# Seven products of a layer added up in shared PSUM banks, and relu, bias and residual in one VectorE instruction

## The chip, the cores and the metric

The kernel runs on one core of one Trainium2 chip. The metric is the device time of one execution in microseconds (us). One more execution is recorded by the profiler, and all views come from that one.

## The reference

There are 32 batches of 512 channels by 1024 nodes. Layer 0 is a graph attention, layer 1 a linear map over the channels; each has a residual and a layernorm over the 1024 nodes.

```python
q = einsum('c,bcn->bn', wq, x);  k = einsum('c,bcn->bn', wk, x)
scores = q[:, None, :] + k[:, :, None]
scores = where(scores > 0, scores, 0.01 * scores)
att = softmax(scores, axis=-1)
agg = einsum('bcn,bmn->bcm', x, att)
y = relu(einsum('oc,bcm->bom', adj, agg) + bm[None, :, None])
x = layernorm(x + y, axis=-1)                 # layer 0
W = adj * adj
x = layernorm(x + einsum('bnf,nm->bmf', x, W) + bias, axis=-1)   # layer 1
```

## The kernel before

**Layer 0 without a 1024 x 1024 softmax.** The leaky relu makes a score's exponential one of two products, depending on whether q + k is positive. If the nodes are sorted by q, a node needs one prefix sum and one suffix sum of weighted columns. Per batch the kernel does this:

- `project` multiplies `x` by the weights in eight steps of 128 nodes (matmuls `zp`, L274); ACT copies each result to `zrow` (L262).
- `peak` and `spread` find the largest q (L287, L305) and spread q over all partitions by eight transposes (L298) and one more, `mx` (L302).
- `place` finds each node's rank by comparing with all others (`lt`, L331) and turns ranks to row numbers `ranki` (L336); `send` scatters the rows to a table in DRAM in the order of q (indirect DMA of POOL, L341). `count` finds each node's place for -k on ACT (L356).
- `fetch` reads the sorted rows back to `zs` (DMA, issued by SP, L389). `weigh` builds weights (`w`, L403, and `lq`, L411). `table` forms prefix and suffix sums in nine steps: PE (`tp`, L431), an ACT copy (`ts`, L436), one-row copies of carried sums back to `zs` by POOL (L440) and by ACT (L442), and stores of `ts` to DRAM by SP. A step needs the row that the step before copied.
- `pick` gathers for each node its row of the table (indirect DMA of POOL, L452) to `rows`; `shares` works out its mixing factors (from L471); `scale` (ACT, L498) and `gain` (DVE, L506) mix the three parts.
- `turn` transposes the result on PE (`op`, L544); ACT adds the bias and takes the relu (L548) to `y`; `add` adds the residual `x` on DVE (L553); `stats` (L515), `root` (POOL, L523, L524), `shift` (L530) and `apply` (ACT, L536) are the layernorm.

**Layer 1 by seven products.** W (with the identity for the residual) and Y, the output of layer 0, are cut into 2 x 2 quarters, and seven products of quarters take the place of eight. The sums of weight quarters S1 to S4 are made once. Those of Y are made per batch by `sums` (L589): T1 = Y12 − Y11, T2 = Y22 − T1, T3 = Y22 − Y12, T4 = Y21 − T2. The output's upper rows (tiles 0 and 1) are called `u`, its lower ones `v`, the column halves `lo` and `hi`:

- 11 (`u` lo) = A11·Y11 + A12·Y21
- 12 (`u` hi) = A11·Y11 + S2·T2 + S1·T1 + S4·Y22
- 22 (`v` hi) = A11·Y11 + S2·T2 + S3·T3 + S1·T1
- 21 (`v` lo) = A11·Y11 + S2·T2 + S3·T3 + A22·T4

Each product is two parts `m` of 128 rows, each of two fp32 matmuls over 128 x 512 (L605). It fills two PSUM banks, one tile of the pool `ps_mm` that has three. VectorE (DVE) adds the products up as they come, 128 x 512 at a time (L617), with the bias in the first reads: 18 reads per batch in nine kinds, of which `u4` and `22` read no PSUM. The bias of the right half has that of the left half subtracted, since the left half's sums carry it on.

**The order.** It is written out by hand, every engine runs its instructions in that order, and semaphores join them. A slot `s` works on four batches: `project` for batch s+2, the table for s+1, `turn` and layer 1 for s, the output's layernorm and stores for s−1. After the projection `phase(s)` follows: layer 1 of `s`, with ranks and sends of s+2, the last table step and the gathers of s+1 between its parts. `mul[0]` to `mul[13]` are the fourteen half products on PE in the order A11, S1, S2, S3, A22, S4, A12. POOL's transfers go p0 p1 s0 s1 p2 p3 s2 s3 p4 p5 s4 s5 p6 s6 s7 p7 (p a gather, s a send), then SP issues the fetch. The first and last batches have orders of their own (`begin`, `opening`, `end`). In the last two batches the sums T4 (of 30) and T3, T4 (of 31) and one kind of addition (of 31) run on POOL.

Buffers: `x` has 12 tiles of 128 x 1024, `y` four and `v`, the output before it is stored, four. The tiles of `v` for tiles 2 and 3 of the old batch are normalised and stored at the beginning of `phase`, and are filled again by the batch of that slot. T1 to T4 lie in parts of `rows` that are free at the time.

Of the kernel before, what the change touches and what calls it, by code (L numbers as in the profile page):

```python
# [23 lines left out]
def gat_gcn_resnorm_kernel(  # L24
# [11 lines left out]

# [18 lines left out]
    xpool = ctx.enter_context(tc.tile_pool(name="xpool", bufs=12))  # L89
    tpool = ctx.enter_context(tc.tile_pool(name="tpool", bufs=3))  # L90
    ypool = ctx.enter_context(tc.tile_pool(name="ypool", bufs=4))
    vpool = ctx.enter_context(tc.tile_pool(name="vpool", bufs=4))
# [16 lines left out]
    vec = const.tile([3 * CT, P], F32, name="vec")  # L109
# [4 lines left out]
    bm_sb = const.tile([P, CT], F32, name="bm_sb")  # L114
# [44 lines left out]
    xs = {}  # L159
    kept = {}  # L160

    def load(b, ct):
        xt = xpool.tile([P, N], F32, name=f"x_{b}_{ct}", tag="x")
        nc.sync.dma_start(out=xt, in_=x[b, ct * P : (ct + 1) * P, :])
        xs.setdefault(b, []).append(xt)
# [26 lines left out]
    def turn_weights():  # L192
# [4 lines left out]
        nc.vector.tensor_copy(bm_sb, pt[:, 2 * CT : 3 * CT])  # L197
# [17 lines left out]
    def square_weights():  # L215


        nc.vector.tensor_tensor(w1, adj_sb, adj_sb, ALU.mult)
        for ct in range(CT):
            nc.vector.tensor_tensor(  # L220
                w1[:, ct, ct * P : (ct + 1) * P], w1[:, ct, ct * P : (ct + 1) * P], ident, ALU.add
            )
        nc.vector.tensor_tensor(ws[:, 0], a21, a22, ALU.add)
        nc.vector.tensor_tensor(ws[:, 1], ws[:, 0], a11, ALU.subtract)
        nc.vector.tensor_tensor(ws[:, 2], a12, ws[:, 1], ALU.subtract)
        nc.vector.tensor_tensor(a21, a11, a21, ALU.subtract)
        nc.vector.tensor_tensor(bias_bc[:, hi], bias_bc[:, hi], bias_bc[:, lo], ALU.subtract)
# [11 lines left out]
    room = {  # L239
        ("T1", 0): (5, 2), ("T2", 0): (5, 0), ("T2", 1): (5, 1),  # L240
        ("T1", 1): (6, 0), ("T3", 1): (6, 2), ("T3", 0): (6, 1),
        ("T4", 0): (7, 0), ("T4", 1): (7, 2),
    }

    info = {}
    ys = {}
    vs = {}
# [18 lines left out]
    def project(b, nt, part, kept=True):  # L266
# [5 lines left out]
        for ct in range(part * CT // 2, (part + 1) * CT // 2):  # L272
            for h in range(2):
                nc.tensor.matmul(  # L274
                    zp[:, h, 0:CE],
                    xb[ct][:, nt * P : (nt + 1) * P],
# [16 lines left out]
    def spread(b, to="lq"):  # L293
# [13 lines left out]
        if to == "v":  # L307
            qs = vpool.tile([P, N], F32, name=f"qs_{b}", tag="v")
# [15 lines left out]
    def place(b, *some):  # L324
# [10 lines left out]
        n0, n1 = some[0], some[-1] + 1  # L335
# [164 lines left out]
    def gain(b, some):  # L500

        g, ra = mixes[b]
        for k in some:
            u = g[:, k, 1, 1 : C + 1]
            for i in (2, 0):
# [3 lines left out]
            us.setdefault(b, []).append(u)  # L509
# [30 lines left out]
    def turn(b, ot, pool=ps_mm):  # L540
# [6 lines left out]
        t = ypool.tile([P, N], F32, name=f"y_{b}_{ot}", tag="y")  # L547
        nc.scalar.activation(t, op, AF.Relu, bias=bm_sb[:, ot : ot + 1])  # L548
        ys.setdefault(b, []).append(t)

    def add(b, ot):
        t = ys[b][ot]
        nc.vector.tensor_tensor(t, t, xs[b][ot], ALU.add)  # L553

    def settle(b, ot):
# [3 lines left out]
        stats((0, b, ot), ys[b][ot])  # L559
# [7 lines left out]
    def quarter(b, name, a):  # L567

        if b < B - 2:
            k, u = room[name, a]  # L570
            return rows[:, k, u * ZW : u * ZW + H]
        if (b, name) not in kept:
            kept[b, name] = vpool.tile([P, N], F32, name=f"{name}_{b}", tag="v")
        return kept[b, name][:, a * H : (a + 1) * H]

    def sums(b, *some):

        yt = ys[b]
        for name, a in some:
            t, t1 = quarter(b, name, a), quarter(b, "T1", a)  # L580
            t2 = quarter(b, "T2", a) if name in ("T2", "T4") else None
            y1, y2 = yt[a], yt[CT // 2 + a]
            of, less = {
                "T1": (y1[:, hi], y1[:, lo]), "T2": (y2[:, hi], t1),
                "T3": (y2[:, hi], y1[:, hi]), "T4": (y2[:, lo], t2),
            }[name]
            on_pool = ("T4",) if b == B - 2 else ("T3", "T4") if b == B - 1 else ()
            by = nc.gpsimd if name in on_pool else nc.vector
            by.tensor_tensor(t, of, less, ALU.subtract)  # L589

    def layer1(b):


        yt = ys[b]

        def part(name, a):
            if name[0] == "Y":
                return yt[(CT // 2) * (name[1] == "2") + a][:, lo if name[2] == "1" else hi]
            return quarter(b, name, a)

        def make(w, y, m, some=range(CT // 2)):
            if 0 in some and (m == 0 or b == B - 1 and w in ("S4", "A12")):
                ops[b, w] = ps_mm.tile([P, 2, H], F32, name=f"o{w}_{b}_{m}", tag="mm")
            for a in some:
                nc.tensor.matmul(  # L605
                    ops[b, w][:, m, :], quarters[w][:, a, m * P : (m + 1) * P], part(y, a),
                    start=(a == 0), stop=(a == CT // 2 - 1),
                )

        def read(mt, half, w, m, *of):  # L610
            if (b, mt) not in vs:
                pool, tag = (xpool, "x") if b >= B - 2 else (vpool, "v")
                vs[b, mt] = pool.tile([P, N], F32, name=f"v_{b}_{mt}", tag=tag)
            x0 = ops[b, w][:, m, :] if w else vs[b, mt][:, half]
            x1 = bias_bc[:, half] if not of else vs[b, of[0]][:, of[1]]
            by = nc.gpsimd if b == B - 1 and not w and half is hi and of[1] is lo else nc.vector
            by.tensor_tensor(vs[b, mt][:, half], x0, x1, ALU.add)  # L617

        mul, get = [], {}
        for w, y in (  # L620
            ("A11", "Y11"), ("S1", "T1"), ("S2", "T2"), ("S3", "T3"),
            ("A22", "T4"), ("S4", "Y22"), ("A12", "Y21"),
        ):
            for m in range(2):
                mul.append(lambda *some, w=w, y=y, m=m: make(w, y, m, *some))
        for m in range(2):
            u, v = m, 2 + m
            for name, what in (
                ("c1", (u, lo, "A11", m)),
                ("c5", (v, hi, "S1", m)),  # L630
                ("u2", (u, hi, "S2", m, u, lo)),
                ("u3", (v, lo, "S3", m, u, hi)),
                ("u4", (u, hi, None, m, v, hi)),
                ("22", (v, hi, None, m, v, lo)),
                ("21", (v, lo, "A22", m, v, lo)),
                ("12", (u, hi, "S4", m, u, hi)),
                ("11", (u, lo, "A12", m, u, lo)),
            ):
                get[name, m] = lambda what=what: read(*what)

        def reads(*names):
            for name in names:
                for m in range(2):
                    get[name, m]()

        return mul, get, reads

    def stats1(b, *some):
        for mt in some:
            stats((1, b, mt), vs[b, mt])  # L650
# [13 lines left out]
    def store(b, mt):  # L664
        nc.sync.dma_start(out=out[b, mt * P : (mt + 1) * P, :], in_=vs.pop((b, mt)))

    def rest(b, after):

        mul, get, reads = layer1(b)
        names = (("c1",), ("c5",), ("u2",), ("u3", "u4", "22"), ("21",), ("12",), ("11",))  # L670
        for i in range(len(mul)):
            mul[i]()
            if i == 0:
                shift(0, b, CT - 1)
                apply(0, b, CT - 1)
                sums(b, ("T2", 0), ("T2", 1), ("T3", 0), ("T3", 1), ("T4", 0), ("T4", 1))
            for name in names[i // 2]:
                if b == B - 1 and i > 9:
# [381 lines left out]
```

## Time and profile before

| | |
|---|---|
| device time, three runs | 2321.87, 2324.4, 2327.32 us; median 2324.4 |
| profiled execution: span | 2323.5 us, 30952 instructions |
| PE busy | 2206.9 us, 95% |
| PE weight load busy | 1388.3 us, 60% |
| DVE busy | 2003.3 us, 86% |
| ACT busy | 1403.0 us, 60% |
| POOL busy | 1042.8 us, 45% |
| DMA | 548.68 MB, mean 236 GB/s |
| mean granted PE clock | 0.978 |

The profiled execution's own time is its span, 2323.5 us, from its first to its last instruction. Busy shares are averages over the whole execution, with an opening of some 160 us and an end of about the same length in which engines wait for each other. A group's mean duration counts an instruction from start to end; neighbours on an engine overlap a little, so what an instruction costs its engine is the distance from one start to the next.

### The profile page before, as it was taken

To read this page: it belongs to the slowest core of one execution; us is meant where nothing else is said; L and a number is where in the kernel's file an instruction comes from. 1 tells how busy PE (TensorE), PEld (TensorE's weight loads), DVE (VectorE), ACT (ScalarE), POOL (GpSimd) and SP (SyncE) were. 2 spreads that over 40 slices of the span, in tenths; PEclk is the share of its full clock that TensorE was granted. 3 is DMA by queue.
4 is the path that set the end of the run, shared out by engine and by line. 5 is a ranking of instruction groups with operands and counts; after the bars stand their busy time and mean duration, and the time that the engine had idled before them with its cause. 6 is when DMAs were issued, how large, how long until landed. Compare 5 with 4: busy or idle time off the path is not lost.

```text
span 2323.5 us, 30952 instructions
## 1 busy us (share of the span) xinstructions
PE 2206.9 (95%) x9521; PEld 1388.3 (60%) x9521; DVE 2003.3 (86%) x4153; ACT 1403.0 (60%) x2185; POOL 1042.8 (45%) x1296
## 2 busy tenths in 40 slices
PE   8969999999999999999999999999999999999775
PEld 7636666566665656666656665656666665666332
DVE  4278989888998988899988898998899888889777
ACT  2665566666556667566667556666656666755543
POOL 2424444544444544444453444454444454444433
PEclk9979999999999999999999999999999999999877
DMA  6657878777878777787877787877777877777741
GB/s 250 200 165 238 261 239 280 245 222 235 252 242 265 257 230 231 241 263 248 270 238 220 239 257 240 274 257 224 227 248 253 260 257 231 227 239 248 235 164 73
DMA packets 175421, 548.68 MB, mean 236 GB/s; under 512 B 24748, under 2 KB 24760, under 8 KB 175256
## 3 DMA queue, kind: packets, MB, share of 16 engines
q1 hardware_dynamic: 117888, 277.18, 40.3%
q0 software_dynamic: 57344, 269.52, 33.2%
q8 instruction: 76, 1.25, 0.2%
q14 instruction: 89, 0.73, 0.1%
q10 hardware_dynamic: 24, 0.01, 0.0%
HBM read 338.17 MB, written 208.43 MB: 235 GB/s over the span
## 4 chain that ended last, share of the span: by engine, by line
DVE 42%; DMA 19%; PE 16%; issue 7%; POOL 6%; ACT 6%; SPq 2%; POOLq 0%; DVEq 0%; ACTq 0%
DVE lt L331 12%; DVE v L617 9%; DMA zs<-td 8%; PE zp L274 8%; DVE st L515 6%; PE tp L431 5%; DMA td<-zrow,ranki 5%; DMA rows<-td,idx 4%; DVE rows L589 4%; DVE rows L506 3%; DVE y L553 2%; POOL td L341 2%; PE op L544 2%; DMA td<-ts 2%; SPq L389 2%
## 5 line engine op out<-in xcount | busy, mean ns | idle before, releaser
L274 PE MATMUL zp<-wmT,x 128*128 128x257 f32 x4096 | 947.7, 383 | 1.4 <-ACT zrow L262 1.3
L274 PEld LDWEIGHTS zp<-wmT,x 128*128 128x128 f32 x4096 | 757.5, 190 | 163.4 <-issue 36.8
L440 POOL COPY zs<-ts 1x513 f32<-1x513 f32 x251 | 191.2, 762 | 676.3 <-ACT ts L436 675.3
L431 PE MATMUL tp<-zs,lq 128*64 128x257 f32 x2304 | 333.2, 404 | 63.5 <-DVE lq L411 24.8
L506 DVE SCALAR_TENSOR_TENSOR rows<-rows,ra 128x512 f32<-128x512 f32 x512 | 379.4, 762 | 11.7 <-ACT rows L498 2.5
L452 POOL DMA_INDIRECT rows<-td,idx x256 | 291.9, 1140 | 204.0 <-issue 115.8
L341 POOL DMA_INDIRECT td<-zrow,ranki x256 | 279.0, 1090 | 119.7 <-DVE ranki L336 46.6
L331 DVE SCALAR_TENSOR_TENSOR lt<-qb,zrow,first 128x1024 int8<-128x1024 f32 x240 | 307.1, 1280 | 4.3
L474 ACT ACTIVATE ac<-s 128x4 f32<-128x4 f32 x64 | 13.3, 208 | 486.4 <-DVE s L473 387.9
L431 PEld LDWEIGHTS tp<-zs,lq 128*64 128x64 f32 x2304 | 153.3, 140 | 224.6 <-POOL zs L440 82.5
L356 ACT ACTIVATE sg<-lq,kc 128x1024 int8<-128x1024 f32 x240 | 275.1, 1146 | 6.8
L605 PE MATMUL oA<-y,adj_sb 128*128 128x512 f32 x512 | 243.8, 609 | 11.0 <-ACT y L536 9.9
L436 ACT COPY ts<-tp 128x514 f32<-128x514 f32 x288 | 168.4, 585 | 110.5 <-PE tp L431 85.5
L605 PE MATMUL oS<-rows,ws 128*128 128x512 f32 x480 | 210.9, 591 | 0.0
L498 ACT ACTIVATE rows<-rows,ra 128x512 f32<-128x512 f32 x256 | 166.8, 711 | 55.7 <-DVE ra L485 50.2
L262 ACT COPY zrow<-zp 128x514 f32<-128x514 f32 x256 | 144.8, 577 | 84.1 <-PE zp L274 76.6
L523 POOL TENSOR_SCALAR rs<-mv 128x1 f32<-128x1 f32 x256 | 88.6, 346 | 237.7 <-DVE mv L517 140.6
L553 DVE TENSOR_TENSOR y<-y,x 128x1024 f32<-128x1024 f32 x128 | 156.1, 1219 | 45.1 <-ACT y L548 45.1
L536 ACT ACTIVATE y<-y,nb,rs 128x1024 f32<-128x1024 f32 x128 | 158.5, 1238 | 54.5 <-DVE nb L530 53.2
L524 POOL TENSOR_TENSOR rs<-rs,mhalf 128x1 f32<-128x1 f32 x256 | 180.4, 705 | 21.4
L515 DVE BATCH_NORM_STATS2 st<-y 128x6 f32<-128x512 f32 x256 | 163.8, 681 | 2.7 <-issue 0.2
L605 PEld LDWEIGHTS oA<-y,adj_sb 128*128 128x128 f32 x512 | 94.1, 195 | 120.5 <-issue 98.1
(119 smaller groups left out, 2640.5 us busy)
## 6 DMA issues: line engine op xcount, KB each, us to landing
x<-in_x_dram SPq DMA_DIRECT2D x128, 512.0 KB
out_dram<-v SPq DMA_DIRECT2D x126, 512.0 KB
td<-ts SPq DMA_DIRECT2D x512, 120.5 KB
zs<-td SPq DMA_DIRECT2D x64, 602.3 KB
zs<-td SPq DMA_DIRECT2D x64, 240.9 KB
zs<-td SPq DMA_DIRECT2D x96, 120.5 KB
td<-ts SPq DMA_DIRECT2D x64, 96.4 KB
td<-zs SPq DMA_DIRECT2D x8, 514.0 KB
```

Source lines behind the costliest of these rows:

```text
L274: nc.tensor.matmul(zp[:, h, 0:CE], xb[ct][:, nt * P : (nt + 1) * P], wmT[:, ct, h * CE : (h + 1) * CE], start=(ct == 0), stop=(ct == CT - 1),)
L331: nc.vector.scalar_tensor_tensor(lt, qs, zrow[:, nt, 0:1], first[:, o : o + N], ALU.subtract, ALU.is_lt, accum_out=rank[:, nt : nt + 1],)
L341: sc = nc.gpsimd.indirect_dma_start(out=td[:, :], out_offset=bass.IndirectOffsetOnAxis(ap=ranki[:, nt : nt + 1], axis=0), in_=zrow[:, nt, ...
L356: nc.scalar.activation(sg, qs, AF.Sign, bias=kc[:, nt : nt + 1], accum_out=sgn[:, nt : nt + 1])
L431: nc.tensor.matmul(tp[i * G : (i + 1) * G, h, 0:CE], lw[:, ks[i], :], zs[:, j, h * CE : (h + 1) * CE], start=True, stop=True,)
L440: by.tensor_copy(zs[0:1, to, 1:ZW], ts[0:1, 1:ZW])
L452: nc.gpsimd.indirect_dma_start(out=rows[:, mt, :], out_offset=None, in_=tds[b].rearrange("(s u) c -> s (u c)", u=3), in_offset=bass.Indire ...
L506: nc.vector.scalar_tensor_tensor(u, g[:, k, i, 1 : C + 1], ra[:, k, i : i + 1], u, ALU.mult, ALU.add)
L515: nc.vector.bn_stats(st[:, h, :], t[:, h * H : (h + 1) * H])
L553: nc.vector.tensor_tensor(t, t, xs[b][ot], ALU.add)
L605: nc.tensor.matmul(ops[b, w][:, m, :], quarters[w][:, a, m * P : (m + 1) * P], part(y, a), start=(a == 0), stop=(a == CT // 2 - 1),)
L617: by.tensor_tensor(vs[b, mt][:, half], x0, x1, ALU.add)
```

## The change

Products that are needed together are added in PSUM. Bank pair A takes A11·Y11, then S2·T2, S3·T3 and A22·T4 on top; B takes S1·T1, then S4·Y22; C takes A12·Y21. DVE reads a partial sum between two products, so the next product on the pair waits for that read. Each of the seven reads spans both parts (128 x 2 x 512): `p1` (A), `p5` (B), `u2` (A), `22` (A), `12` (B), `11` (C), `21` (A). The order on PE becomes A11, S1, S2, S4, S3, A12, A22. The sums T1 to T4 are one instruction each over two row tiles (128 x 2 x 512); T3 overwrites Y12 and T4 overwrites Y11. The subtraction of the left half's bias is gone.

ACT's relu (L548) is gone. DVE computes max(op, −bm) + x from PSUM in one instruction; this is relu(op + bm) + x less bm, and bm, one number for a row of 1024 nodes, is taken out by the layernorm's mean.

`gain` does one of its two mixing steps for all tiles and then the other. `x`, `y` and `v` are single tiles of the same size in place of pools. In `phase` the ranks, sums, reads and gathers are put in another order: POOL's transfers now go p0 p1 s0 s1 p2 p3 s2 s3 p4 s4 s5 p5 s6 s7 p6 p7. All of the last batches' sums and additions run on DVE.

```diff
     def gain(b, some):
         g, ra = mixes[b]
-        for k in some:
-            u = g[:, k, 1, 1 : C + 1]
-            for i in (2, 0):
+        for i in (2, 0):
+            for k in some:
+                u = g[:, k, 1, 1 : C + 1]
                 nc.vector.scalar_tensor_tensor(
                     u, g[:, k, i, 1 : C + 1], ra[:, k, i : i + 1], u, ALU.mult, ALU.add
                 )
...
     def turn(b, ot, pool=ps_mm):
...
-        nc.scalar.activation(t, op, AF.Relu, bias=bm_sb[:, ot : ot + 1])
-        ys.setdefault(b, []).append(t)
+        tops[b, ot] = op
     def add(b, ot):
-        t = ys[b][ot]
-        nc.vector.tensor_tensor(t, t, xs[b][ot], ALU.add)
+        nc.vector.scalar_tensor_tensor(
+            yall[:, ot], tops.pop((b, ot)), nbm[:, ot : ot + 1], xs[b][:, ot], ALU.max, ALU.add
+        )
...
     def sums(b, *some):
-        for name, a in some:
...
-            by.tensor_tensor(t, of, less, ALU.subtract)
+        for name in some:
             of, less = {
+                "T1": ("Y12", "Y11"), "T2": ("Y22", "T1"), "T3": ("Y22", "Y12"), "T4": ("Y21", "T2"),
             }[name]
+            nc.vector.tensor_tensor(part(b, name), part(b, of), part(b, less), ALU.subtract)
     def layer1(b):
+        def make(w, y, at, first, m, some=range(CT // 2)):
+            if 0 in some and first and m == 0:
+                ops[b, at] = ps_mm.tile([P, 2, H], F32, name=f"o{at}_{b}", tag="mm")
             for a in some:
                 nc.tensor.matmul(
+                    ops[b, at][:, m, :], quarters[w][:, a, m * P : (m + 1) * P],
+                    part(b, y)[:, a, :], start=first and a == 0, stop=a == CT // 2 - 1,
+                    skip_group_check=not first,
                 )
+        def read(at, of, half, seen, m=None):
+            to, o = v[:, row[of], half], ops[b, at]
+            more = to if seen else bias_bc[:, half].unsqueeze(1).to_broadcast([P, 2, H])
+            if m is not None:
+                to, o, more = to[:, m, :], o[:, m, :], more[:, m, :]
+            nc.vector.tensor_tensor(to, o, more, ALU.add)
+        for of in (
+            ("A11", "Y11", "A", True), ("S1", "T1", "B", True), ("S2", "T2", "A", False),
+            ("S4", "Y22", "B", False), ("S3", "T3", "A", False), ("A12", "Y21", "C", True),
+            ("A22", "T4", "A", False),
+        ):
...
+            "p1": ("A", "u", lo, False), "p5": ("B", "v", hi, False), "u2": ("A", "u", hi, False),
+            "12": ("B", "u", hi, True), "22": ("A", "v", hi, True), "11": ("C", "u", lo, True),
+            "21": ("A", "v", lo, False),
...
     def phase(s, mid, new, old):
...
         mul[1]()
         pick(mid, 0)
         pick(mid, 1)
-        rank(0, 1)
+        rank(0)
+        mul[2]()
+        mul[3]()
+        sums(s, "T2")
+        read("p1")
+        rank(1)
         send(new, 0)
         send(new, 1)
-        sums(s, ("T2", 0), ("T2", 1))
-        mul[2]()
-        mul[3]()
         pick(mid, 2)
         pick(mid, 3)
-        get["c1", 0]()
-        rank(2, 3)
+        mul[4]()
+        mul[5]()
+        rank(2)
+        read("p5")
+        rank(3)
         send(new, 2)
         send(new, 3)
         if new < B - 1:
             pick(mid, 4)
-        sums(s, ("T3", 0), ("T3", 1))
-        get["c1", 1]()
-        mul[4]()
-        mul[5]()
-        sums(s, ("T4", 0), ("T4", 1))
+        mul[6]()
+        mul[7]()
+        sums(s, "T3")
+        rank(4)
+        read("u2")
+        mul[8]()
+        mul[9]()
+        rank(5)
+        send(new, 4)
+        send(new, 5)
         if new < B - 1:
             pick(mid, 5)
-        reads("c5")
-        rank(4, 5)
-        send(new, 4)
-        send(new, 5)
-        mul[6]()
-        mul[7]()
+        rank(6)
+        rank(7)
+        send(new, 6)
+        send(new, 7)
+        sums(s, "T4")
         if new < B - 1:
             pick(mid, 6)
-        reads("u2")
-        rank(6, 7)
-        send(new, 6)
-        send(new, 7)
-        mul[8]()
-        mul[9]()
-        if new < B - 1:
             pick(mid, 7)
         fetch(new)
-        reads("u3", "u4", "22")
         mul[10]()
         mul[11]()
-        reads("21")
+        read("22")
         mul[12]()
         mul[13]()
+        read("12")
+        read("11")
         shares(mid, 0, NT // 2)
         scale(mid, range(NT // 2))
-        reads("12")
+        read("21")
         gain(mid, (0, 1))
-        reads("11")
         gain(mid, (2, 3))
```

## The prediction

> **What bounds the kernel now.** I read the table of stretches first, then the waits, the groups, and last one slot's timeline on TensorE (PE) and VectorE (DVE). Four steady stretches of 72.6 us (core 0; then span, busy us and instructions of PE, PEld, DVE, ACT, POOL; clock, DMA share, GB/s):
>
> ```profile
> 1000.00:1072.60 72.60, 72.29 (x309) 44.80 (x308) 66.71 (x137) 44.21 (x70) 36.00 (x44) 1.00 0.79 252
> 1072.60:1145.20 72.60, 72.50 (x310) 44.90 (x309) 66.36 (x140) 43.63 (x68) 35.64 (x44) 1.00 0.79 259
> 1145.20:1217.80 72.60, 70.17 (x305) 43.85 (x305) 64.05 (x137) 43.60 (x69) 34.00 (x43) 1.00 0.78 245
> ```
>
> PE is busy for 97 to 100% at full clock; DVE, which the change relieves, for about 91%. So a gain in a slot can only come from PE's gaps. I measured those from one slot's `mx` transpose (L302) to the next: 29 slots last 68.93 us in the mean. Adding the shortest time that each group of PE instructions ever took gives 67.57, so 1.36 us per slot is all that can be won, 39 us in the run. The waits (engine, line, releaser; us in total, times, longest) name the gaps:
>
> ```profile
> POOL rows L452 <- DMA td<-ts: 67.0, 16, 4.8
> ...
> DVE y L553 <- ACT y L548: 45.1, 48, 3.8
> ...
> PE tp L431 <- DVE lq L411: 24.8, 24, 8.5
> PE tp L431 <- POOL zs L440: 23.3, 37, 3.0
> ```
>
> Per slot, that is 0.39 us before the table's first step (it needs `lq`), 0.43 at its eighth and 0.14 at its fifth (they need POOL's copy of one row to `zs`), 0.24 in layer 1, and crumbs. The relu wait of 45 us stands on DVE, not on PE: it costs only what it passes on.
>
> **The skill and this trace.** (1) "VectorE: DVE Perf Modes", section on the TRN2 errata: an fp32 tensor_tensor takes (N+151)/0.96 ns, 691 at N=512. The groups agree (682), and successive reads start 0.60 us apart, so a merged 1024 pays the fixed part once: 1.135 between starts for such adds here.
>
> ```profile
> L440 POOL COPY zs<-ts 1x513 f32<-1x513 f32 x251 | 191.2, 762 | 676.3 <-ACT ts L436 675.3
> ...
> L553 DVE TENSOR_TENSOR y<-y,x 128x1024 f32<-128x1024 f32 x128 | 156.1, 1219 | 45.1 <-ACT y L548 45.1
> ...
> L548 ACT ACTIVATE y<-op,bm_sb 128x1024 f32<-128x1024 f32 x128 | 141.8, 1109 | 10.9 <-PE op L544 8.7
> L617 DVE TENSOR_TENSOR v<-oS,v 128x512 f32<-128x512 f32 x192 | 122.8, 680 | 0.0
> ```
>
> (2) "SBUF — State Buffer", Who interferes with whom: GpSimd shares a port pair with DVE's second SBUF input, so a DVE operation with two SBUF inputs holds it up. The trace agrees: the L440 copy takes 0.60 us beside bn_stats, 0.99 in the median (1.5 at most) beside L553. (3) "PSUM — Partial Sum Buffer", The four PSUM rules: a partial sum may be read in mid-group if the read is synchronised. Before, every product has its own bank, so no run here shows what it costs PE. (4) "DMA: Bandwidth & Descriptors", Queues: an engine round-robins between queues by packet; the fetch and the gathers will share so.
>
> **The change, part by part.** Times below count from `mx`; L0 is the first rank comparison (L331), `mx`+2.65.
>
> *Relu fused.* 4 ACT instructions of 1.109 go: 4.4 us per slot of ACT, which is 60% busy, so nothing by itself. DVE's add reads PSUM instead of a second SBUF tile; a 128x1024 form with PSUM is not in the trace; between the plain add (1.135) and the rank comparison (1.28), I take 1.20, +0.25 per slot. POOL's copy loses its rival: 0.99 to 0.60, so the waits at the eighth and fifth steps, 0.57 together, mostly go: **−0.55** per slot (ends: 0 if another DVE operation takes its place, −0.6). The buffers `op` are now freed by DVE later than by ACT; their next users (the seventh projection among them) have 1.5 us to spare, so 0.
>
> *Layer 1's sums and reads.* Before, 18 DVE reads x 0.60 = 10.8 us; after, 7 x about 1.135 = 7.95: −2.85. Eight sums of 0.60 become four of 1.135: −0.26. Gains in two passes: an STT (L506) followed by a dependent one starts its successor after 0.777 us, an independent one after 0.669, so 8 x 0.108 = −0.86. With the +0.25 DVE loses **3.7 of about 65.7 us** per slot. What of that reaches PE? In the slot at 1120.23, PE (start, us):
>
> ```profile
> 1120.23 0.27 PE L302 MATMUL mx<-ident,q 128*128 128x128 f32 x1
> ...
> 1124.99 7.03 PE L605 MATMUL oS<-rows,ws 128*128 128x512 f32 x16
> 1132.06 3.70 PE L605 MATMUL oS<-rows,adj_sb 128*128 128x512 f32 x8
> 1135.60 3.60 PE L605 MATMUL oA<-rows,adj_sb 128*128 128x512 f32 x8
> ```
>
> and DVE:
>
> ```profile
> 1122.86 1.28 DVE L331 SCALAR_TENSOR_TENSOR lt<-qb,zrow,first 128x1024 int8<-128x1024 f32 x1
> ...
> 1133.12 1.28 DVE L617 TENSOR_TENSOR v<-oS,bias_bc 128x512 f32<-128x512 f32 x2
> ...
> 1145.76 0.15 DVE L471 TENSOR_TENSOR s<-rows,kc 128x4 f32<-128x4 f32 x1
> ```
>
> PE runs a product in 3.43 us (8 x 0.429). After the change products wait for *reads*, since A11, S2, S3, A22 share bank pair A and S1, S4 share B. I laid DVE's new order out from L0 (rank 1.32, ranki 0.08, merged operation 1.15): T2 done 2.65, `p1` 3.8, `p5` 7.7, T3 10.2, `u2` 12.7, T4 18.0, `22` 19.2. PE finishes S1 at 5.56, S2 8.99, S4 12.42. So S2 waits for `p1` not at all, S4 not for `p5`, A22 not for `22`; only S3 misses `u2`, by 0.3 plus two hand-overs of 0.15: 0.6 in place of the 0.24 gap: **+0.36** (ends 0, +0.7).
>
> `p5` writes the buffer from which the old batch's last row tile is stored. That store's last packet lands at `mx`+8.87 in most slots, at 9.4 to 10.6 in 9 of 26; `p5` would start at 9.3. A later landing delays `p5`, the ranks, sends and `u2` queued behind it on DVE, and PE at S3, up to 1.75 us more in one slot of four: **+0.4** in the mean (ends 0, +1.7 if every slot's store is late).
>
> *POOL's and SP's queues.* POOL issues 16 indirect transfers per slot, 1.33 to 1.41 apart, from the landing of the last table store to about `mx`+29.4. That wait stays. Sends 6 and 7 now precede picks 6 and 7, so the last send is issued 1.33 earlier and SP starts the fetch (L389) 1.3 to 2 earlier, while the last picks still move. Pick 7 keeps its issue time and lands at 35.2; sharing the 16 engines I put it 0.5 later (ends 0, +1.0). The second L471, 0.7 after that landing, waits for it: DVE's savings before it are lost in that wait. From there to `lq` only the shorter gains count, −0.21. So the table's first step comes by PE's path at 41.85 (43.6 in the bad quarter), by DVE's at 41.9 − 0.21 + 0.5 = 42.2; later of the two, mean **42.5**, against 41.9 now. From there to the next `mx` 27.0 becomes 26.45. Period 68.95 against 68.93: **0 per slot** (ends −0.6, +0.9), x 29.
>
> *Opening and end,* where PE waits for chains. Opening: relu wait off batch 0's chain (1.1) and shorter sums and gains: −2 (−1 to −4). End: in the last tables, copies and sends leave DVE's tail, −2; relu off, −1.1; batch 30's layer 1, from its last normalisation to batch 31's first add 30.7 us, loses about 3.0 of DVE time; the last batch's layer 1, 36.3, about 1.0. Together −7 (−4 to −10). T3 and T4 of the last batches and the adds of batch 31 move from POOL to DVE, counted in these.
>
> Sum against the profiled span 2323.5 (0.9 below the median of the three runs, 2324.4): 0 − 2 − 7 = −9, hence **2315** on the median's scale.
>
> **The rivals.**
> A (above, chance 0.40): 2315, own range 2307 to 2322.
> B, the relief reaches PE: picks land no later and stores are in time, so the first step comes at 41.9 and the period falls by 0.55 to 0.6: −17 − 9 gives 2298. For: PE's gaps at steps five and eight are real and their cause goes. Against: two new couplings sit just where there is no slack. Chance 0.20.
> C, slower: `p5` stands behind the output store in most slots, and S3 behind `u2`. With `p5` late by 1.4 us everywhere PE comes to the first step at 43.25, period +0.77: +22 − 9 gives 2337. Behind `p5` on DVE stand the rank comparisons that SP's fetch and POOL's sends need, behind S3 on PE the last two products. It decides from a first step later than `mx`+42.8 (+0.31 per slot, which uses up the 9). For: the landing is already within 0.4 us of `p5`. Against: 17 of 26 slots land at 8.87. Chance 0.26.
> D, no change that shows: PE's own work sets the slot, and the end's gains are half of what I count while the slots lose 0.15 each: 2324 within 0.2% (4.65 us, about what a measurement of this kernel can tell from no change). Chance 0.14.
> That the relu's wait of 45 us is won in full is excluded by PE's load of 97 to 100%: its gaps hold 39 us in all.
>
> **The numbers.** Faster by over 0.2%: B, and 0.36 of A's 0.40, 0.56. Within 0.2%: D and the rest of A, 0.18. Slower: C, 0.26. Cases of both signs matter, so A's own range stands above; the range 2291 to 2336 reaches through most of B and to the middle of C, leaving 0.2 out.
>
> **What would show it.** In the profile after: DVE's busy time down by 3 to 4 us and ACT's by 4 to 4.5 per slot; the L440 copy's mean from 762 to near 620 ns and PE's waits for it mostly gone; a new wait of PE's S3 product on a DVE read of about 0.6 us per slot, and none at S2, S4 and A22; `p5` waiting for the output store in a minority of slots; the fetch starting 1.3 us or more earlier, the second L471 about 0.5 later. Wrong if the S3 wait is near 2 us in most slots (C), if the first step of the table stays at 41.9 (B), or if the copies stay slow, for then my −0.55 is missing and the period is +0.5.

## The result and the profile after

The changed kernel takes 2337.84 us in the median of 7 runs (2331.15 to 2343.88), the kernel before 2324.4 (7 runs). The ratio is 1.0054, with a 95% interval of 1.0039 to 1.007: slower by half a per cent. The profiled span went from 2323.5 to 2337.0 us. The forecast was 2315, faster.

The same stretches as before, of the kernel after (core 0; span, busy us and instructions of PE, PEld, DVE, ACT, POOL; clock, DMA share, GB/s):

```profile
1000.00:1072.60 72.60, 68.67 (x299) 43.05 (x299) 58.92 (x116) 40.60 (x66) 33.55 (x44) 1.00 0.79 245
1072.60:1145.20 72.60, 72.33 (x310) 44.95 (x309) 62.94 (x124) 39.40 (x64) 33.80 (x42) 1.00 0.79 247
1145.20:1217.80 72.60, 71.02 (x306) 44.20 (x305) 61.31 (x117) 39.41 (x64) 34.33 (x43) 1.00 0.78 249
```

Single rows vary with what falls in them. Over 508 us (1000 to 1508.2) PE fell from 501.4 to 494.4 us of busy time, DVE from 460.0 to 423.4, ACT from 311.8 to 280.4. So the two engines were relieved as planned and PE, the bound, works less densely. The waits of the kernel after say for whom (us in total, times, longest):

```profile
DVE s L431 <- DMA rows<-td,idx: 137.7, 30, 6.8
...
PE tp L391 <- DVE lq L371: 23.7, 29, 7.7
PE zp L230 <- ACT zrow L218: 21.9, 23, 2.8
...
DVE v L573 <- DMA out_dram<-v: 9.6, 27, 2.1
PE tp L391 <- POOL zs L400: 9.0, 7, 2.9
```

The first and the third of these waits in the kernel before:

```profile
DVE s L471 <- DMA rows<-td,idx: 17.7, 21, 4.9
...
PE zp L274 <- ACT zrow L262: 1.3, 1, 1.3
```

The wait for POOL's copy has gone from 23.3 to 9.0 us, as forecast. What is new: DVE stands 137.7 us in `shares` (L431) until gathered rows have landed, and PE stands 21.9 us ahead of a projection because ACT has not emptied a PSUM tile. One slot shows that these are one chain. Its `mx` starts at 1124.30. DVE, ACT and PE in that slot, one fence each (start, us; what ended the idle time ahead of it in brackets):

```profile
1151.55 5.38 DVE L466 SCALAR_TENSOR_TENSOR rows<-rows,ra 128x512 f32<-128x512 f32 x8
1161.65 0.16 DVE L431 TENSOR_TENSOR s<-rows,kc 128x4 f32<-128x4 f32 x1 [4.72 <-DMA rows<-td,idx]
...
1167.23 0.48 DVE L371 TENSOR_TENSOR lq<-tri,w 128x128 f32<-128x128 f32 x2
```

```profile
1162.23 0.21 ACT L434 ACTIVATE ac<-s 128x4 f32<-128x4 f32 x1 [7.76 <-DVE s L433]
1163.30 1.33 ACT L458 ACTIVATE rows<-rows,ra 128x512 f32<-128x512 f32 x2 [0.86 <-DVE ra L445]
1164.54 0.57 ACT L218 COPY zrow<-zp 128x514 f32<-128x514 f32 x1
```

```profile
1139.80 3.70 PE L561 MATMUL oA<-y,adj_sb 128*128 128x512 f32 x8 [0.28 <-DVE v L573]
...
1165.16 2.00 PE L230 MATMUL zp<-wmT,x 128*128 128x257 f32 x8 [0.88 <-ACT zrow L218]
1167.57 1.28 PE L391 MATMUL tp<-zs,lq 128*64 128x257 f32 x8 [0.40 <-DVE lq L371]
```

DVE is done with its gains early and then waits 4.72 us for the last gather. Its factors release ACT's exponential (L434), behind which stand two scalings and then the copy that frees the PSUM tile; PE starts its fifth projection at 1165.16, at the end of that copy. The table's first step then waits 0.40 for `lq`, which DVE makes after the gains. In the kernel before, in the slot at 1120.23, the same L471 came 36.26 after `mx`; here L431 comes 37.35 after it:

```profile
1156.49 0.16 DVE L471 TENSOR_TENSOR s<-rows,kc 128x4 f32<-128x4 f32 x1 [0.91 <-DMA rows<-td,idx]
```

Means of 26 steady slots, in us after `mx`, measured by the same rule in every trace. A gather has landed when the last packet of its rows has ended, and is issued when POOL's instruction for it has ended; `lq`, `shares` and the step are taken at their starts:

| | before | after | difference |
|---|---|---|---|
| last send issued by POOL | 28.13 | 26.61 | −1.52 |
| fetch issued by SP | 33.82 | 32.14 | −1.68 |
| last gather issued | 29.49 | 29.30 | −0.19 |
| last gather landed | 35.24 | 36.28 | +1.04 |
| second `shares` (L471, L431) | 35.92 | 37.30 | +1.38 |
| `lq` | 41.76 | 42.89 | +1.13 |
| first step of the table | 42.11 | 43.30 | +1.19 |
| from there to the next `mx` | 26.82 | 26.32 | −0.50 |
| period | 68.93 | 69.62 | +0.69 |

The profiled executions split into opening (to the third `mx`), 29 slots and end: before 156.8 + 1999.5 + 167.2, after 151.3 + 2020.0 + 165.8. So −5.5 + 20.5 − 1.5 = +13.5, the difference of the spans.

The last gather is issued as before. The two ahead of it are not: in the same 26 slots gather 5 is issued at 24.00 instead of 20.85 and gather 6 at 27.96 instead of 25.50.

### The profile page after: what moved, and what is told of

It is laid out like the page before. It is cut to its first block, busy times and chain, and to the rows that moved or that the text cites. A ratio compares the mean times of both kernels' runs of the same rounds, so it can differ in the third digit from the quotient of the medians.

```text
span 2337.0 us, 30261 instructions
## 1 busy us (share of the span) xinstructions
PE 2206.2 (94%) x9521; PEld 1387.7 (59%) x9521; DVE 1875.0 (80%) x3684; ACT 1270.3 (54%) x2057; POOL 1008.3 (43%) x1288
## 4 chain that ended last, share of the span: by engine, by line
PE 39%; issue 22%; DVE 21%; POOL 8%; DMA 5%; ACT 4%; SPq 0%; DVEq 0%; POOLq 0%; ACTq 0%
PE zp L230 17%; PE tp L391 11%; DVE lt L287 8%; DVE v L573 7%; PE op L505 5%; POOL td L301 3%; POOL rows L412 3%; DVE y L550 2%; PE oA L561 2%; ACT y L497 2%; POOL zs L400 2%; DMA rows<-td,idx 1%; PE qb L254 1%; DMA zs<-td 1%; ACT ts L396 1%
## 5 line engine op out<-in xcount | busy, mean ns | idle before, releaser
L230 PE MATMUL zp<-wmT,x 128*128 128x257 f32 x4096 | 951.3, 384 | 22.0 <-ACT zrow L218 21.9
L230 PEld LDWEIGHTS zp<-wmT,x 128*128 128x128 f32 x4096 | 759.1, 190 | 185.2 <-issue 42.2
L400 POOL COPY zs<-ts 1x513 f32<-1x513 f32 x251 | 177.4, 707 | 803.3 <-ACT ts L396 786.8
L561 PE MATMUL oA<-y,adj_sb 128*128 128x512 f32 x768 | 361.7, 607 | 20.4 <-ACT y L497 7.7
L412 POOL DMA_INDIRECT rows<-td,idx x256 | 285.8, 1116 | 206.1 <-issue 123.2
L466 DVE SCALAR_TENSOR_TENSOR rows<-rows,ra 128x512 f32<-128x512 f32 x512 | 346.9, 744 | 2.4 <-ACT rows L458 2.4
L301 POOL DMA_INDIRECT td<-zrow,ranki x256 | 285.9, 1117 | 120.1 <-issue 52.3
L434 ACT ACTIVATE ac<-s 128x4 f32<-128x4 f32 x64 | 13.3, 208 | 485.0 <-DVE s L433 417.0
L561 PEld LDWEIGHTS oA<-y,adj_sb 128*128 128x128 f32 x768 | 139.8, 192 | 201.4 <-issue 158.7
L485 POOL TENSOR_TENSOR rs<-rs,mhalf 128x1 f32<-128x1 f32 x256 | 164.6, 643 | 21.3
L512 DVE SCALAR_TENSOR_TENSOR y<-op,nbm,x 128x1024 f32<-128x1024 f32 x128 | 163.4, 1276 | 3.6 <-PE op L505 3.6
L484 POOL TENSOR_SCALAR rs<-mv 128x1 f32<-128x1 f32 x256 | 95.4, 373 | 158.1 <-DVE mv L478 76.4
L402 ACT COPY zs<-ts 1x513 f32<-1x513 f32 x256 | 157.7, 616 | 8.2
```

What stands on the lines that cost most here:

```text
L230: nc.tensor.matmul(zp[:, h, 0:CE], xb[:, ct, nt * P : (nt + 1) * P], wmT[:, ct, h * CE : (h + 1) * CE], start=(ct == 0), stop=(ct == CT - 1),)
L301: sc = nc.gpsimd.indirect_dma_start(out=td[:, :], out_offset=bass.IndirectOffsetOnAxis(ap=ranki[:, nt : nt + 1], axis=0), in_=zrow[:, nt, ...
L400: by.tensor_copy(zs[0:1, to, 1:ZW], ts[0:1, 1:ZW])
L412: nc.gpsimd.indirect_dma_start(out=rows[:, mt, :], out_offset=None, in_=tds[b].rearrange("(s u) c -> s (u c)", u=3), in_offset=bass.Indire ...
L466: nc.vector.scalar_tensor_tensor(u, g[:, k, i, 1 : C + 1], ra[:, k, i : i + 1], u, ALU.mult, ALU.add)
L561: nc.tensor.matmul(ops[b, at][:, m, :], quarters[w][:, a, m * P : (m + 1) * P], part(b, y)[:, a, :], start=first and a == 0, stop=a == CT ...
```

## The experiments

Two theories stood against each other. **G**: the last gathers land later, because they stand behind the sends and share the DMA engines with a fetch that now starts earlier. **S**: PE's new wait ahead of the product S3, where it needs the read `u2` (0.52 us per slot, and 0.09 ahead of S4; both are taken from the starts of the products, which lie 3.43 us apart when nothing waits).

### POOL's old order in the changed kernel (e1)

```diff
-            u = rows[:, 5 + i, :].rearrange("p (u c) -> p u c", u=3)
+            u = rows[:, (5, 7)[i], :].rearrange("p (u c) -> p u c", u=3)
...
+            pick(mid, 5)
         send(new, 4)
         send(new, 5)
-            pick(mid, 5)
         rank(6)
         rank(7)
+            pick(mid, 6)
         send(new, 6)
         send(new, 7)
         sums(s, "T4")
-            pick(mid, 6)
             pick(mid, 7)
```

> The changed kernel with POOL's old order of transfers (gather 5 before sends 4 and 5, gather 6 before sends 6 and 7, gather 7 last); T2 lies in tile 7 of rows instead of tile 6, so that gather 6 need not wait for T4. Theory G (the late gathers cost it: in the trace after, the last gather lands 1.0 us later after mx, the second L471 comes 1.4 later, lq 1.1 and the first step of the table 1.2): landing back from 36.3 to about 35.2, first step back from 43.3 to 42.0, period from 69.6 to 68.4 or less, time about 2337 - 29 x 1.2 = 2302. Rival S (PE's product S3 waits for u2, 0.5 us per slot): that wait is not touched, time stays at 2337 within 4.

Measured: 2308.39 us, ratio to before 0.9934 (0.9921 to 0.9946). The last gather lands at 35.08, the second `shares` comes at 35.82, the first step at 42.00, the period is 68.43. The same waits as above:

```profile
DVE s L431 <- DMA rows<-td,idx: 99.9, 30, 5.9
...
PE tp L391 <- DVE lq L371: 19.6, 19, 8.5
...
PE zp L230 <- ACT zrow L218: 2.8, 3, 1.6
```

G holds and S does not: PE's wait ahead of S3 is nearly as it was (0.45 us), and the 29 us came from the order of the gathers (with T2 in another tile, which that order needs). DVE still waits 99.9 us for gathers in this kernel. That wait is DVE being early; only the landing's time counts.

### POOL's new order in the kernel before (e3)

```diff
-        if new < B - 1:
-            pick(mid, 5)
         reads("c5")
         rank(4, 5)
         send(new, 4)
         send(new, 5)
+        if new < B - 1:
+            pick(mid, 5)
...
-        if new < B - 1:
-            pick(mid, 6)
...
         if new < B - 1:
+            pick(mid, 6)
             pick(mid, 7)
```

> The kernel before with POOL's new order alone: gather 5 after send 5, gathers 6 and 7 after send 7. Theory G: last gather lands 1.0 later, first step of the table 1.2 later, time about 2324 + 29 x 1.0 = 2353. Rival S, for which the gathers' place does not matter: 2324 within 4.

Measured: 2353.43 us, ratio 1.013 (1.0115 to 1.0145); landing 36.16, first step 43.37, period 69.81. With no other part of the change the order alone costs 29 us. The waits of this kernel:

```profile
DVE s L471 <- DMA rows<-td,idx: 58.7, 30, 7.3
...
PE tp L431 <- DVE lq L411: 32.2, 31, 8.9
...
PE zp L274 <- ACT zrow L262: 23.3, 23, 2.4
```

PE's wait for ACT's copy, 1.3 us before, is there as in the changed kernel.

### Why the gather lands later: the fetch held back (e2)

```diff
             pick(mid, 7)
+            nc.sync.dma_start(out=held, in_=rows[0:1, 7, 0:8])
         fetch(new)
```

> The changed kernel, in which a 32-byte DMA that reads what the last gather wrote stands on SP ahead of the fetch, so that the fetch starts only when the last gather has landed. Only the landing is asked for. Theory G1 (the fetch, 1.7 us earlier than before, shares the DMA engines with the last gathers): the last gather lands at about 35.2 after mx as in the kernel before. Theory G2 (gathers 6 and 7 stand behind the sends, so their bytes are queued late, fetch or no fetch): it still lands at 36 or later. The time itself gets worse under both, by 1.5 to 3 us per slot (about 2380 to 2420), because the weights then wait for the fetch.

Measured: the fetch is issued at 36.18, and the last gather lands at 35.44, with all transfers of POOL in the changed kernel's order. So the fetch's share of the DMA engines (G1) is up to 0.84 of the 1.04 us, and at least 0.2 remain for bytes that are queued later (G2). The split is no sharper than that, for two reasons. First, the fetch overlapped the last gather in the kernel before too, and e2 takes this away as well: by the DMA packets of the traces, 44 KB of the fetch have come in per slot when the last gather lands in the kernel before, 386 KB in the kernel after and none in e2. Second, the gathered rows do come later without the fetch: 33 us after `mx`, 419 KB of them are still to come in the kernel before, 647 in the kernel after and 602 in e2. The old order with the fetch held back was not run.

The second `shares` is back at 35.95 in e2, where the kernel before has 35.92. In e2 it follows the landing after 0.51 us. In e1, where the fetch is issued 1.4 us ahead of the landing, it is 0.75; in e3 and the kernel after, where that is 4.3 and 4.1, it is 0.99 and 1.02. So the way from the landing to `shares` grows with the fetch's lead.

The time of e2 was 2358.21 us (one run), better than I expected: the weights waited for the fetch, but the first step came at 43.2 and the period was 70.3, not 71 to 73.

### PE's wait ahead of S3 (e4 and e8)

In e4 A12 goes ahead of S4 and S3 on PE:

```diff
-        mul[6]()
-        mul[7]()
+        mul[10]()
+        mul[11]()
         sums(s, "T3")
         rank(4)
-        read("u2")
-        mul[8]()
-        mul[9]()
+        mul[6]()
+        mul[7]()
+        read("u2")
...
         fetch(new)
-        mul[10]()
-        mul[11]()
+        mul[8]()
+        mul[9]()
```

> The changed kernel with the product A12 moved ahead of S4 and S3 on PE, so that p5 and u2 have 3.4 us more before PE needs them. Both theories expect PE's wait ahead of S3 (0.5 us per slot) and ahead of S4 (0.1) to vanish. Rival S: the slot gets shorter by 0.6, time about 2337 - 17 = 2320. Theory G: PE only comes earlier to the table's first step and waits there for lq, time 2337 within 4.

Measured: 2338.13 us, ratio 1.0067 (1.005 to 1.0084), no change against the kernel after. But it tells less than I meant. The waits ahead of S3 and S4 vanished, and a longer one, 1.3 us at a time, came ahead of A22 in their place, since `22` now reads a product that PE makes 3.4 us later:

```profile
PE oA L561 <- DVE v L573: 40.3, 30, 1.7
```

That the time did not rise with it speaks against S, but S3's own wait was not tested so. I tried it in another way. From e5 (below), e8 only puts the read `u2` ahead of the fifth rank comparison on DVE:

```diff
         sums(s, "T3")
-        rank(4)
         read("u2")
+        rank(4)
```

> The kernel e5_end_whole with the read u2 ahead of the fifth rank comparison on DVE. PE's wait ahead of the product S3 (about 0.45 us per slot) should vanish. With the gathers back in place PE and lq come to the first step of the table nearly together (lq at 41.4, step at 42.0), so by theory G only a part of it shows, 0.1 to 0.3 per slot, 3 to 9 us off the time of e5_end_whole; if the wait ahead of S3 counts in full, 13.

Measured: 2305.55 us against 2303.84 for e5, measured together (ratios 0.9905 and 0.9903 to the kernel before; the runs of both lie between 2300 and 2310). The wait ahead of S3 is gone and the first step still comes at 42.2, with `lq` at 41.7. The wait was hidden behind `lq`: of the 13 us that it would have been worth in full, and of the 3 to 9 that I expected, none show. Theory S falls.

### The end: part-wise reads of the last batch (e5)

In the end the kernel after loses what I had not foreseen. Around batch 31's products, PE in the kernel after:

```profile
2300.94 1.88 PE L561 MATMUL oB<-y,ws 128*128 128x512 f32 x4
2308.24 3.78 PE L561 MATMUL oB<-y,ws 128*128 128x512 f32 x4 [5.42 <-DVE x L573]
2311.81 1.99 PE L561 MATMUL oA<-y,adj_sb 128*128 128x512 f32 x4
2314.59 1.98 PE L561 MATMUL oA<-y,adj_sb 128*128 128x512 f32 x4 [0.78 <-DVE x L573]
```

and DVE:

```profile
2306.15 1.23 DVE L476 BATCH_NORM_STATS2 st<-x 128x6 f32<-128x512 f32 x2
2307.42 0.21 DVE L478 BATCH_NORM_AGGREGATE mv<-st 128x2 f32<-128x12 f32 x1
2307.55 0.64 DVE L573 TENSOR_TENSOR x<-oB,x 128x512 f32<-128x512 f32 x1
```

For the last batch each half product is followed by its own read. The other half product goes to the same tile, so it waits for that read; the read at 2307.55 stands behind batch 30's statistics. From e1, e5 reads both parts at once up to `22`:

```diff
-            if b == B - 1 and i > 5:
+            if b == B - 1 and i > 9:
                 read(names[i // 2], i % 2)
...
-            if i in (8, 9):
-                half(i - 6, 1)
+            if i == 9:
+                half(2, 1)
+                half(3, 1)
```

> The kernel e1_gathers_back, in which the last batch reads the products into 12 and 22 over both parts at once (as all other batches do) instead of part by part. In the trace after, the second part of S4 of batch 31 waits 5.4 us for the read of the first part, which stands on DVE behind the statistics of batch 30, and three later half products wait 0.8 us each. If that is the loss of the end: the last batch's layer 1 gets 6 to 7 us shorter, time about 2308 - 6 = 2302. Rival (DVE's own load in the end is the limit, whichever read comes first): 2308 within 2.

Measured: 2303.84 us, ratio 0.9903 (0.988 to 0.9926), against 0.9934 for e1: 7 us. In the traces the end takes 157.9 us instead of 166.3; it is 157.9 to 159.8 in the four kernels with this edit (e5, e7, e8, e11), and 165.8 to 166.3 in the kernel after, e1, e2 and e4. The slots of e1 and e5 are the same code, and yet their periods in the two traces are 68.43 and 68.79: a difference of 0.3 us per slot between two single traces says nothing by itself.

### The fused relu, undone and alone (e6 and e9)

From e1, e6 puts the relu back on ACT:

```diff
-        tops[b, ot] = op
+        nc.scalar.activation(yall[:, ot], op, AF.Relu, bias=bm_sb[:, ot : ot + 1])
...
-        nc.vector.scalar_tensor_tensor(
-            yall[:, ot], tops.pop((b, ot)), nbm[:, ot : ot + 1], xs[b][:, ot], ALU.max, ALU.add
-        )
+        nc.vector.tensor_tensor(yall[:, ot], yall[:, ot], xs[b][:, ot], ALU.add)
```

> The kernel e1_gathers_back with the relu and bias on ACT again and the residual as a VectorE addition of two SBUF tensors (the fused instruction undone, all else kept). Theory P (the gain of the fused form is POOL's one-row copy to zs, which an addition with two SBUF inputs holds up): the copies beside the addition go from 0.60 back to about 1.0 us, PE's waits at the table's fifth and eighth step come back, period +0.4 to +0.5, time about 2308 + 13 = 2321. Rival Q (the fused form gains because DVE no longer waits for ACT, wherever that is): the waits at those two steps stay small, and the period grows elsewhere or not at all; 2308 within 4 if not at all.

Measured: 2351.97 us, ratio 1.011 (1.0088 to 1.0131); the period is 69.80, 1.37 us per slot above e1's. That is three times what I expected. 0.90 of it is PE's wait ahead of the table's eighth step; the rest is spread over small waits. POOL ahead of that step, in e6:

```profile
847.33 1.25 POOL L486 TENSOR_SCALAR rs<-mv 128x1 f32<-128x1 f32 x1 [1.54 <-ACT y L499]
848.67 1.40 POOL L487 TENSOR_TENSOR rs<-rs,mhalf 128x1 f32<-128x1 f32 x1
850.02 0.60 POOL L402 COPY zs<-ts 1x513 f32<-1x513 f32 x1
```

and in e1:

```profile
837.49 1.25 POOL L484 TENSOR_SCALAR rs<-mv 128x1 f32<-128x1 f32 x1 [1.53 <-ACT y L497]
838.82 0.57 POOL L485 TENSOR_TENSOR rs<-rs,mhalf 128x1 f32<-128x1 f32 x1
839.34 0.60 POOL L400 COPY zs<-ts 1x513 f32<-1x513 f32 x1
```

The victim is not the copy (0.60 in both) but the power in front of it (L487, in e1 L485; the second instruction of `root`), which takes 1.40 instead of 0.57 us beside the addition with two SBUF inputs, in all of the 26 slots. The first line takes 1.25 us in both, beside the sum T1, which also has two SBUF inputs and is one long instruction since the change. So theory P has the right mechanism with another instruction as its main victim; ahead of the fifth step it is the copy after all, 0.91 us in the mean against 0.61 in e1.

e9 makes the same fusion in the kernel before, and nothing else:

```diff
-        nc.scalar.activation(t, op, AF.Relu, bias=bm_sb[:, ot : ot + 1])
+        tops[b, ot] = op
...
-        nc.vector.tensor_tensor(t, t, xs[b][ot], ALU.add)
+        nc.vector.scalar_tensor_tensor(
+            t, tops.pop((b, ot)), bm_sb[:, ot : ot + 1], xs[b][ot], ALU.max, ALU.add
+        )
```

> The kernel before with relu, bias and residual in one VectorE instruction from PSUM and nothing else changed. Theory P (two SBUF inputs of the addition held up POOL): PE's waits at the table's fifth and eighth step (0.14 and 0.43 per slot) go, period 68.93 to about 68.4; with 2 to 4 us from opening and end, 2324 - 15 - 3 = 2306. If the fused form was worth more only because it stood beside the merged sum T1 in e6_relu_on_act (1.35 per slot), the gain here is near 0.55 per slot and not 1.35; at 1.35 the time would be 2282.

Measured: 2293.29 us, ratio 0.9874 (0.9859 to 0.9889), 29 us faster. The copy to `zs`, 762 ns in the mean before:

```profile
L440 POOL COPY zs<-ts 1x513 f32<-1x513 f32 x251 | 158.4, 631 | 737.1 <-ACT ts L436 737.1
```

Per slot 0.91 us went: 0.55 at the fifth and eighth step as expected, and 0.33 ahead of the fourth product in layer 1, where DVE had been late. The opening gave 4.8 us, the end 5.0. I had expected 0.55 and 3 us.

### Sends first (e10, e7, e12)

POOL waits at the beginning of each phase for the last table store. e10 puts two sends into that time, in the kernel before:

```diff
-        pick(mid, 0)
-        pick(mid, 1)
         rank(0, 1)
         send(new, 0)
         send(new, 1)
+        pick(mid, 0)
+        pick(mid, 1)
```

> The kernel before with sends 0 and 1 ahead of gathers 0 and 1 on POOL and nothing else changed. Theory G: the last gather lands about 1.3 earlier (as in e7_sends_first), lq comes before PE, which is at the first step at about 41.5 instead of 42.1: -0.4 to -0.5 per slot, time about 2324 - 13 = 2311; the waits at the fifth and eighth step stay. If the first step were bound by PE in any case: 2324 within 4.

Measured: 2304.94 us, ratio 0.9923 (0.9907 to 0.9938). The last gather lands at 34.26 instead of 35.24, the first step comes at 41.62, the period is 68.29. Of the 0.64 us per slot, 0.36 are PE's wait ahead of the first step.

e7 is e8 with that order (`rank(0)`, `rank(1)` and the two sends ahead of gathers 0 and 1).

> The kernel e8_u2_early with ranks 0 and 1 and their sends ahead of gathers 0 and 1. POOL stands idle there until the last table store has landed (8.2 us after mx), so two of the sixteen transfers go out in idle time and the last gather is issued 2.7 us earlier. Theory G (the last gather's landing sets lq, and with it the first step of the table): landing about 1.5 to 2.5 earlier, first step bound by PE alone at about 41.5, period 67.7 to 68.0, time 2308 - 6 - 29 x 0.55 = 2286. Rival (the DMA engines are full from 8 to 35 us, so the landing moves by little whatever is issued when, or the sends delay the landing of the table stores): as e8_u2_early within 5.

Measured: 2276.01 us, ratio 0.9785 (0.9763 to 0.9807). The landing is at 33.87, `lq` at 40.31, and the first step at 41.43 now waits for PE alone. The period is 67.55.

e11 gives e7 the old order of `gain`:

```diff
-        for i in (2, 0):
-            for k in some:
-                u = g[:, k, 1, 1 : C + 1]
+        for k in some:
+            u = g[:, k, 1, 1 : C + 1]
+            for i in (2, 0):
```

> The kernel e7_sends_first with the old order of gain (both steps of a tile, then the next tile). DVE gets 0.8 us per slot more to do, 0.2 to 0.4 of it ahead of lq. There lq now comes about 1.1 before PE is at the first step, so by theory G nothing of it shows: 2276 within 4. If DVE's load as such counts: 0.8 x 29, about 2299.

Measured: 2277.4 us, ratio 0.9803 (0.9789 to 0.9816): no difference from e7, though `lq` comes at 40.66 instead of 40.31. Where PE is the bound, DVE's 0.8 us per slot have no price.

e12 is e9 and e10 together, with the old layer 1.

> The kernel e9_before_fused with sends 0 and 1 ahead of gathers 0 and 1: both good edits on the old layer 1, with its seven separate products and eighteen reads. In e9 lq binds the first step at 41.7; in e10 PE came to it at 41.6, and in e9 PE arrives some 0.3 earlier than there, so the first step comes at about 41.35 and the period is about 67.65: 2293 - 29 x 0.37 = 2282. If shared banks and merged reads bring something of their own once lq no longer binds, this kernel stays clearly behind e7_sends_first (2276) by more than 4; if not, it is within 4 of it apart from the difference of the ends (162.3 in e9 against 159.0 in e7).

Measured: 2275.63 us, ratio 0.9772 (0.9748 to 0.9796), as fast as e7. Two stretches each, first of e12, then of e7:

```profile
1000.00:1072.60 72.60, 72.60 (x326) 47.02 (x324) 67.30 (x140) 43.85 (x73) 30.93 (x40) 1.00 0.80 251
1072.60:1145.20 72.60, 72.60 (x330) 46.78 (x328) 66.26 (x137) 42.22 (x70) 33.97 (x45) 1.00 0.77 241
```

```profile
1000.00:1072.60 72.60, 72.60 (x324) 47.36 (x323) 61.41 (x126) 41.49 (x68) 29.82 (x40) 1.00 0.77 250
1072.60:1145.20 72.60, 72.60 (x326) 46.67 (x325) 63.14 (x124) 43.45 (x72) 30.84 (x41) 1.00 0.77 245
```

PE has no gap left in these stretches. DVE has 4.5 us more to do per stretch in e12, and it costs nothing. Once PE is full, the shared banks and merged reads bring no time of their own. With the old place of sends 0 and 1 the new layer 1 even stands behind: e1, which has it with the fusion and POOL's old order, is at 0.9934, e9 without it at 0.9874, 14 us. In the traces e1 loses 14.7 us to e9 in the 29 slots, 4.0 at the end (166.3 against 162.3, which e5's edit takes back) and 0.8 in the opening. The two also differ in the order of ranks, sums and reads and in `gain`, and no run takes the shared banks alone, so which part of the new layer 1 costs the slots is open.

## Why the prediction was wrong

- **What bounds the kernel.** Right: PE does, and a slot could only win its 1.36 us of gaps. e7 and e12 won all of it, with periods of 67.55 and 67.51 against the floor of 67.57, which was thus a hair too high.
- **DVE and ACT.** Right: DVE 4.4 us less per slot (3.7 forecast; 90.5% of 68.93 became 83.3% of 69.62), ACT 3.9 less (4.4), each a little outside the span that I had named as a sign.
- **Fused relu.** Right in kind and place: from the table's first step to the next `mx` 0.50 us went (0.55 forecast). Its worth was under-sized: I let the relu's wait on DVE pass on nothing more, and e9 shows 0.33 per slot in layer 1 and 10 us in opening and end besides. The Trainium skill's "SBUF — State Buffer", Who interferes with whom, has a VectorE instruction with two SBUF inputs contend with a GpSimd instruction that reads SBUF; the trace agrees once more, with the power's 1.40 against 0.57 us in e6. The mean of the copy fell only to 707 ns after the change, not to 620; e9, with the same fusion, has 631.
- **S3's wait.** The size was right (0.36 more forecast; 0.52 came ahead of S3 and 0.09 ahead of S4, and the old 0.24 ahead of the fourth product went: net 0.37). As forecast, S2 and A22 start 3.43 us after the product ahead of them, without a wait, although DVE reads their bank pair in between. `p5` waited for the output store 27 times, in most slots and not in the minority that I had named, but for 9.6 us in all, 0.33 per slot on DVE (on PE I had taken 0.4; 0.09 arrived there). e8 showed what I had not counted on: no part of it that the runs can tell from noise reaches the time while `lq` is later.
- **The failed step** is the one on POOL's and SP's queues. I wrote that the last gather lands 0.5 later, ends 0 and +1.0. I had followed gather 7 alone, whose issue does not move, and not gathers 5 and 6, issued 3.15 and 2.46 us later. The last gather landed 1.04 later, at the end of my range, and the second `shares` followed it after 1.02 instead of 0.68 us, where I had 0.7. So the table's first step came at 43.3 where I had 42.5, from a base of 42.1 where I had read 41.9: 1.19 us later instead of 0.6. Over 29 slots that difference is 17 of the 20 us by which the slots, entered with 0 in the sum, came out longer. e3 shows it without any other part of the change, e1 its removal, e2 that the fetch's sharing is up to 0.84 of the 1.04. The Trainium skill's "DMA: Bandwidth & Descriptors", Queues, rings and completion order, has each DMA engine take packets of its queues in turn; e2's 0.84 us fits that, though no run here shows the turns themselves. What I lacked was a size.
- **The path to PE.** I had PE wait for `lq` alone. It first waits for ACT's copy of an earlier projection, queued behind the exponential that needs the gather: 21.9 us in all, against 1.3. In the slot shown it adds nothing to the time, because `lq` comes later still; no run takes this wait away alone.
- **Opening and end.** −5.5 where I had −2, −1.5 where I had −7. Up to batch 31's last residual addition the end went better than forecast: it came 8.8 us earlier, where I had 6.1. Then the last batch's layer 1, for which I had −1.0, took 43.5 us instead of 36.2. I counted DVE's work there and missed that reads part by part make the next half product wait. e5 took that back.
- **The rivals.** C, slower, gave the right side and 2337, but by luck: its mechanism did not decide (`p5` behind the store, S3 behind `u2`). Its test did point right: a first step later than 42.8. B's condition, a landing no later than before, was met by e1, at 2308 us where I had 2298.

## What to carry to other kernels

Where one engine is full, price a change by the event that this engine waits for last, here the landing of one gather, and follow every transfer that the change moves past another to that event; relief of other engines is worth nothing until it reaches it. A reordering that comes along with a change deserves its own line in the sum: here it cost 29 us while the part in the title that looked larger, the shared banks, was worth nothing once PE was full. Take the parts of a change one at a time: the fusion, with two sends moved into POOL's idle time, gives 2275.63 us with the old layer 1.

## What was not expected of the hardware

A GpSimd instruction on 128 x 1 elements took 1.40 us instead of 0.57 beside a VectorE addition of two SBUF tensors (e6, L487), so the size of an instruction says little on how long such a neighbour holds it. A fetch on another queue that overlapped the last gathers moved the landing of a 128-row gather by 0.84 us (e2 against the kernel after), although the gather was issued at the same time (29.2 and 29.3 us after `mx`).
